# The graph layer turned round: normed tokens as weights, 256 adjacency rows moving, and the linear product afterwards

## The chip, the cores and the metric

The kernel runs on one core of a Trainium2 chip. The metric is the device time of one execution, in microseconds (us). Engines are named as in the profile: PE is TensorE (PEld its weight loads), DVE is VectorE, ACT is ScalarE, POOL is GpSimd, SP is SyncE, which here issues DMAs.

## The reference, cut to what matters

There are 4096 tokens of 256 features and a dense 4096 x 4096 adjacency matrix. One graph layer is followed by one layer of causal attention and a mixture of eight experts, two of them for each token. The change touches the graph layer alone:

```
f = layernorm(x)
h = f @ neigh_W.T
deg = adj.sum(axis=1, keepdims=True) + 1.0
h = adj @ h / deg
x = x + concatenate([f, h], axis=-1) @ lin_W.T
```

With lin_W split into a left half L1 (for f) and a right half L2 (for h), the update is x + f L1 + (adj f M) / deg, with M = neigh_W.T L2 (in the transposes that the code uses). The product with M may be made before the product with adj or after it.

## The kernel before, in words

The graph stage works on row blocks b and source blocks jb of 512 tokens, eight of each. For every pair the 512 x 512 adjacency block, transposed in memory, is loaded (`load`, three buffers) and multiplied with the features of the source block. The product is done by a seven-product scheme (Strassen's, in Winograd's form): the adjacency block is cut into quarters A11 to A22, `halve` makes four sums of them on VectorE (S1, S2, S4, and S3 in place of A21; lines L428 to L431), and the features are cut and combined in the same way (tile g with G11, G12, G21, G22, T1, T2, T3 in the place of G12, and T4; L453 to L456). Each sum tile has two slots, used in turn.

In the kernel before, `features(b)` multiplies the normed tokens, transposed by `turned_x` (L377, copied by L381), with 512 columns at once: M in the left half, L1 in the right (L439). ACT copies the left half of the result into g (L446), VectorE adds the right half to the residual (L449).

`aggregate(b, steps)` is the main loop. For each jb it issues 28 matmuls (L477): seven products, two row tiles t, two halves k of the source tokens. The adjacency piece is the stationary operand (128 x 128) and g the moving one, 128 columns; two of the seven products have a 129th column of ones in g, from which the row sums of the adjacency come out. After the eighth source block the sums are put together from PSUM: an ACT copy (L497) and VectorE operations (L498 to L504), then the degrees (L505 to L507) and the residual (L510), for one t and then the other. The accumulators lie in two PSUM pools of two banks, one pool for each t, so the next row block can only overwrite a bank that has been read.

The order of the work is written out by hand: each engine takes its instructions in the order of the program. The `steps` of a row block are pieces of other work that are put in the middle of a source block. In row block 0 they are `features`, `turned_x`, `halve` and `scales_x` of later blocks. In row block b from 1 on they are the seven or eight parts of `qkv(b - 1)`: `scales` (statistics, and a power on GpSimd, L168 and L169), `norm`, `turn`, four times `rotate` (matmuls L197; ACT's L201, VectorE's L205 and L210, GpSimd's L213 to L217, VectorE's reduction L219 and maximum L220), and four times `turn_heads` (L227 and L232). The last rotation stands in source block 6, the last two turn_heads in source block 7. For b from 1 on, `halve` of the next adjacency block is issued ahead of a source block's matmuls.

After row block 7 the attention stage begins at once on TensorE; it takes over the PSUM banks of the graph stage's pools.

Of the kernel before, what the change touches and what calls it, by code (L numbers as in the profile page):

```python
# [66 lines left out]
def fast_kernel(  # L67
# [170 lines left out]
    with (  # L238
# [20 lines left out]
        for h in range(2):  # L259
# [7 lines left out]
        ml_sb = qT[6]  # L267
        nc.scalar.dma_start(
            ml_sb[:, :, C : 2 * C], lin_t[0:C, :].rearrange("(c p) o -> p c o", p=P)
        )  # L270
# [66 lines left out]
        def fold():  # L337
            for c in range(2):
                pm = p_pj.tile([P, 512], F32, tag="pj", name=f"pm_{c}")
                for k in range(2):  # L340
                    nc.tensor.matmul(
                        pm[:, :C], wn_sb[:, k, c * P : (c + 1) * P], l2_sb[:, k, :],
                        start=(k == 0), stop=(k == 1),
                    )
                nc.scalar.copy(ml_sb[:, c, 0:C], pm[:, :C])
# [14 lines left out]
        g = [gw.tile([P, 7, 2, HC + 1], F32, name=f"g{b}") for b in range(NB)]  # L360
# [5 lines left out]
        AT = {  # L366
            1: (0, 0, HC), 2: (0, HC, HC), 6: (0, 2 * HC, HC), 7: (0, 3 * HC, HC),
            3: (1, 0, HC + 1), 5: (1, HC + 1, HC + 1), 4: (1, 2 * HC + 2, HC),
        }

        def transposed(src, dst):

            for h in range(2):
                tr = p_tr.tile([P, 2, 2, P], F32, tag="tr", name="tr")
                for t in range(2):
                    for c in range(2):
                        nc.tensor.transpose(  # L377
                            tr[:, c, t, :], src[:, 2 * h + t, c * P : (c + 1) * P], ident
                        )
                cols = slice(h * 2 * P, (h + 1) * 2 * P)  # L380
                nc.scalar.copy(dst[:, :, cols], tr.rearrange("p c t i -> p c (t i)"))  # L381

        inputs, turned = {}, {}

        def scales_x(b, at_a_time=TB):
            for t in range(0, TB, at_a_time):
                some = slice(t, t + at_a_time)
                stats(gx, b, range(TB)[some])
                power(rstd[b][:, some], mv[b][:, some, 1:2], 1.0, EPS_LN)
            nc.gpsimd.memset(g[b][:, G22 : T1 + 1, :, HC : HC + 1], 1.0)  # L390

        def normed_x(b, t):
            if t == 0:
                inputs[b] = gx.tile([P, TB, C], F32, tag="f", name=f"f_{b}", bufs=1)
            normed(inputs[b][:, t, :], b, t, rstd[b][:, t])

        def turned_x(b):
            turned[b] = qT[b % 4]
            transposed(inputs.pop(b), turned[b])
# [3 lines left out]
        more = gs.tile([P, 3, 2, 2 * P], F32, name="more_sums")  # L403
        sums_at = [
            tuple(
                t.rearrange("p (k i) -> p k i", k=2)
                for t in (qT[NB - 1][:, 0], qT[NB - 1][:, 1], kT[NB - 1])
# [4 lines left out]
        rows_at = [  # L412
            vv[NB - 1].rearrange("p (r h) c -> p r h c", r=2),
            gs.tile([P, 2, 2, HC], F32, name="rows_sums"),
        ]

        def halve(n):

            if n == NB * NB:
                return  # L420
            a = blocks.pop(n)
            m = {
                f"A{r + 1}{k + 1}": a[:, 2 * k : 2 * k + 2, r * 2 * P : (r + 1) * 2 * P]
                for r in range(2) for k in range(2)
            }
            m["S1"], m["S2"], m["S4"] = sums_at[n % 2]
            m["S3"] = m["A21"]
            nc.vector.tensor_add(m["S1"], m["A21"], m["A22"])  # L428
            nc.vector.tensor_sub(m["S2"], m["S1"], m["A11"])
            nc.vector.tensor_sub(m["S4"], m["A12"], m["S2"])  # L430
            nc.vector.tensor_sub(m["S3"], m["A11"], m["A21"])  # L431
            halves_of[n] = m

        def features(b):
            fT = turned.pop(b)
            for t in range(TB):
                pj = p_pj.tile([P, 512], F32, tag="pj", name=f"pf_{b}_{t}")
                for c in range(2):
                    nc.tensor.matmul(  # L439
                        pj, fT[:, c, t * P : (t + 1) * P], ml_sb[:, c, :],  # L440
                        start=(c == 0), stop=(c == 1),
                    )
                if b + 1 < NB:
                    normed_x(b + 1, t)
                i = t // 2 * 2
                nc.scalar.copy(  # L446
                    g[b][:, i : i + 2, t % 2, 0:HC], pj[:, 0:C].rearrange("p (h c) -> p h c", h=2)
                )
                nc.vector.tensor_add(res[b][:, t, :], res[b][:, t, :], pj[:, C : 2 * C])  # L449
                if b == 0 and t == 1:  # L450
                    halve(0)
            part = [g[b][:, k, :, 0:HC] for k in range(7)]
            nc.vector.tensor_sub(part[T1], part[G12], part[G11])  # L453
            nc.vector.tensor_sub(part[T3], part[G22], part[G12])
            nc.vector.tensor_sub(part[T2], part[G22], part[T1])
            nc.vector.tensor_sub(part[T4], part[T2], part[G21])  # L456

        def aggregate(b, steps):

            acc = [  # L460
                [pool.tile([P, 512], F32, tag="acc", name=f"acc_{b}_{t}_{k}") for k in range(2)]
                for t, pool in enumerate((p_acc0, p_acc1))
            ]
            for jb in range(NB):
# [3 lines left out]
                order = [(p, t) for p in PRODUCTS for t in range(2)]  # L468
                if jb == 0 and b:
                    load_tables(b - 1)  # L470
                if jb == NB - 1 or b and jb == 0:
                    order = [(p, t) for t in range(2) for p in PRODUCTS]
                for i, ((number, left, right), t) in enumerate(order):
                    bank, at, w = AT[number]
                    for k in range(2):

                        nc.tensor.matmul(  # L477
                            acc[t][bank][:, at : at + w], m[left][:, k, t * P : (t + 1) * P],
                            g[jb][:, right, k, 0:w],
                            start=(jb == 0 and k == 0 and number in (1, 3)),  # L480
# [3 lines left out]
                    if i == 6:  # L484
                        for step in steps.get(jb, ()):
                            step()
                load(b * NB + jb + 3)
            for t in range(2):
                p = {
                    number: acc[t][bank][:, at : at + HC] for number, (bank, at, w) in AT.items()  # L490
                }
                rows = rows_at[t]
                deg = gx.tile([P, 2], F32, tag="deg", name=f"deg_{b}_{t}")

                u2 = u4 = rows[:, 0, 1]
                u3 = rows[:, 1, 1]
                nc.scalar.copy(u2, p[1])  # L497
                nc.vector.tensor_add(rows[:, 0, 0], u2, p[2])  # L498
                nc.vector.tensor_add(u2, u2, p[6])
                nc.vector.tensor_add(u3, u2, p[7])  # L500
                nc.vector.tensor_add(u4, u2, p[5])
                nc.vector.tensor_add(rows[:, 0, 1], u4, p[3])
                nc.vector.tensor_sub(rows[:, 1, 0], u3, p[4])
                nc.vector.tensor_add(rows[:, 1, 1], u3, p[5])  # L504
                nc.vector.tensor_scalar_add(deg[:, 1:2], acc[t][1][:, 2 * HC + 1 : 2 * HC + 2], 1.0)  # L505
                nc.vector.tensor_add(deg[:, 0:1], deg[:, 1:2], acc[t][1][:, HC : HC + 1])
                nc.vector.reciprocal(deg, deg)  # L507
                for r in range(2):
                    x1 = res[b][:, 2 * r + t, :]
                    nc.vector.scalar_tensor_tensor(  # L510
                        x1, rows[:, r].rearrange("p h c -> p (h c)"), deg[:, r : r + 1], x1,
                        op0=ALU.mult, op1=ALU.add,
                    )

        def qkv(b):
# [9 lines left out]
            def norm():  # L525
                made["h0"] = gx.tile([P, TB, C], F32, tag="f", name=f"h0_{b}", bufs=1)
                for t in range(TB):
                    normed(made["h0"][:, t, :], b, t, both[b][:, t])
                made["ratio"] = ratio(gx, b)

            def turn():

                made["hT"] = qT[b]
                transposed(made["h0"], made["hT"])
# [14 lines left out]
            def turn_heads(t):  # L549
# [3 lines left out]
            return {  # L553
                0: [scales], 1: [norm], 2: [turn], 3: [lambda: rotate(0)], 4: [lambda: rotate(1)],
                5: [lambda: turn_heads(0), lambda: rotate(2)],
                6: [lambda: turn_heads(1), lambda: rotate(3)],
                7: [lambda: turn_heads(2), lambda: turn_heads(3)],
            }
# [15 lines left out]
        turned_x(0)  # L574
        features(0)
# [10 lines left out]
        aggregate(0, steps)  # L586
        for b in range(1, NB):
            aggregate(b, qkv(b - 1))
# [4 lines left out]
    with (  # L593
# [11 lines left out]
        p_sc = cycle((p_sc0, p_sc1, p_sc2))  # L605
# [1553 lines left out]
```

## Time and profile before

| | |
|---|---|
| Time, median of 3 runs | 1611.35 us (1609.33 to 1614.71) |
| Span of the profiled execution | 1603.0 us |
| Graph stage in it | from the start to 539.6 us |
| TensorE busy | 1588.4 us (99%) |
| VectorE busy | 1025.0 us (64%) |
| One row block from 1 on | 59.3 us, of which VectorE is busy 37.4 us and GpSimd 11.5 us |
| L477, all products | 3584 matmul records of 128 or 129 columns |
| L439, features | 128 matmul records of 512 columns |

An f32 matmul leaves two records, each with its weight load. A record's own duration (275 ns for L477) holds the passage through the array, in which the next record already runs; what a record costs is read from the chain of waits, as the length of a piece over the number of its records. The profile's slices give the busy share of each engine in tenths, for 40 equal parts of the span.

### The profile page before, as it was taken

What the parts mean: (1) busy time and instruction counts of PE and PEld (TensorE: products, weight loads), DVE (VectorE), ACT (ScalarE), POOL (GpSimd) and SP (SyncE); (2) the same over time, 40 slices, a digit from 0 to 9 for tenths busy, and PEclk for the clock granted to TensorE, in tenths of its full rate; (3) what the DMA queues carried; (4) which work ended last, traced back from release to release, by engine and by line L of the source; (5) the groups of instructions that cost most, each with busy time, mean ns of one, the idle gap of its engine ahead of it and who ended that gap; (6) DMA issues with size and microseconds to landing.
All of it is one profiled execution on the core that took longest, in us unless ns stands there. A gap on an engine that the chain in (4) does not pass through costs nothing.

```text
span 1603.0 us, 25842 instructions
## 1 busy us (share of the span) xinstructions
PE 1588.4 (99%) x9996; PEld 1172.1 (73%) x9996; DVE 1025.0 (64%) x2159; ACT 483.8 (30%) x925; POOL 418.3 (26%) x606
## 2 busy tenths in 40 slices
PE   9999999999999999999999999999999999999997
PEld 6779999999999643444343443337889999999997
DVE  5656756656656668789889788794445544343552
ACT  2120110110110445545545545552212222222221
POOL 1001111111111231254453334322422212222213
PEclk9999999999999999999999999999999999999999
DMA  6324434444435000001010001058756777787783
GB/s 230 99 72 145 159 133 146 151 132 161 136 132 165 4 1 1 13 33 36 18 38 28 14 28 38 20 182 235 237 169 199 233 227 251 225 300 248 232 296 67
DMA packets 68005, 209.80 MB, mean 131 GB/s; under 512 B 14688, under 2 KB 46816, under 8 KB 54240
## 3 DMA queue, kind: packets, MB, share of 16 engines
q1 hardware_dynamic: 54608, 190.05, 35.0%
q0 software_dynamic: 12720, 17.47, 5.6%
q8 instruction: 81, 1.33, 0.4%
q10 hardware_dynamic: 544, 0.52, 0.1%
q14 instruction: 52, 0.43, 0.1%
HBM read 180.81 MB, written 31.42 MB: 132 GB/s over the span
## 4 chain that ended last, share of the span: by engine, by line
PE 89%; DVE 7%; ACT 1%; issue 1%; POOL 1%; DMA 0%; SPq 0%; DVEq 0%; POOLq 0%; ACTq 0%
PE acc L477 25%; PE h L1231 20%; PE ya L652 11%; PE sc L617 11%; PE ye_y L1283 5%; DVE sum L640 4%; PE pf L439 3%; PE ye_y L1202 3%; PE pq L197 2%; PE ye_ms L1202 2%; PE po L687 2%; PE tx L1140 1%; ACT pt L622 1%; DVE rden L671 1%; PE trq L227 1%
## 5 line engine op out<-in xcount | busy, mean ns | idle before, releaser
L640 DVE TENSOR_TENSOR sum<-sum,pt 128x1024 f32<-128x1024 f32 (+3 forms) x258 | 295.4, 1145 | 17.2
L622 ACT ACTIVATE pt<-sc 128x1024 f32<-128x1024 f32 (+3 forms) x288 | 252.3, 958 | 173.6 <-PE sc L617 123.8
L477 PE MATMUL acc<-g,a 128*128 128x128 f32 x2048 | 255.9, 275 | 0.0
L617 PE MATMUL sc<-qT_all,kT 64*128 64x512 f32 (+3 forms) x1152 | 250.4, 569 | 1.4 <-ACT pt L622 0.4
L652 PE MATMUL ya<-pt,vv 128*64 128x512 f32 (+3 forms) x1152 | 242.6, 563 | 0.0
L477 PEld LDWEIGHTS acc<-g,a 128*128 128x128 f32 x2048 | 241.9, 192 | 0.0
L1231 PE MATMUL h<-xT,qT_all 128*128 128x256 f32 (+1 forms) x1232 | 221.3, 338 | 0.0
L1231 PEld LDWEIGHTS h<-xT,qT_all 128*128 128x128 f32 x1232 | 196.6, 191 | 20.2 <-issue 1.2
L617 PEld LDWEIGHTS sc<-qT_all,kT 64*128 64x128 f32 x1152 | 103.8, 186 | 141.0 <-issue 106.2
L1238 DVE TENSOR_TENSOR hT<-si,h 128x256 f32<-128x256 f32 (+2 forms) x126 | 62.7, 506 | 189.3 <-ACT si L1237 189.2
L652 PEld LDWEIGHTS ya<-pt,vv 128*64 128x64 f32 x1152 | 76.3, 136 | 146.9 <-issue 139.1
L1303 POOL DMA_INDIRECT acc_dram<-y,rows x57 | 89.7, 1574 | 307.5 <-DVE y L1298 152.3
L1237 ACT ACTIVATE si<-h 128x256 f32<-128x256 f32 (+2 forms) x126 | 57.0, 453 | 278.6 <-PE h L1231 274.6
L1231 PE MATMUL h<-xT,res_all 128*128 128x256 f32 (+1 forms) x616 | 108.2, 334 | 0.0
L1231 PEld LDWEIGHTS h<-xT,res_all 128*128 128x128 f32 x616 | 96.6, 191 | 9.0
L836 POOL DMA_INDIRECT lists<-row,slots x64 | 72.3, 1130 | 115.4 <-issue 114.8
L477 PE MATMUL acc<-g,more_sums 128*128 128x129 f32 (+1 forms) x768 | 101.7, 275 | 0.2 <-DVE more_sums L430 0.2
L477 PEld LDWEIGHTS acc<-g,more_sums 128*128 128x128 f32 x768 | 94.6, 192 | 4.3 <-issue 0.4
L624 POOL TENSOR_SCALAR_AFFINE_SELECT pt<-pt 128x256 f32<-128x256 f32 x64 | 47.6, 770 | 114.1 <-ACT pt L622 113.9
L477 PE MATMUL acc<-g,qT_all 128*128 128x128 f32 (+1 forms) x512 | 74.0, 275 | 0.0
L213 POOL TENSOR_TENSOR ro<-ro,r 128x192 f32<-128x192 f32 x28 | 16.5, 589 | 214.0 <-DVE r L210 214.0
L477 PEld LDWEIGHTS acc<-g,qT_all 128*128 128x128 f32 x512 | 66.4, 192 | 3.9
(275 smaller groups left out, 1960.9 us busy)
## 6 DMA issues: line engine op xcount, KB each, us to landing
a<-in_adj_dram SPq DMA_DIRECT2D x64, 1024.0 KB, 4.9
qT_all<-in_w_dram SPq DMA_DIRECT2D x28, 1408.0 KB, 8.1
res_all<-in_w_dram SPq DMA_DIRECT2D x28, 768.0 KB, 5.3
res_all<-in_w_dram SPq DMA_DIRECT2D x14, 1408.0 KB, 8.4
qT_all<-in_w_dram SPq DMA_DIRECT2D x14, 768.0 KB, 5.1
rows<-lists SPq DMA_DIRECT2D x25, 265.0 KB, 2.9
lists<-pad SPq DMA_DIRECT2D x8, 662.5 KB, 14.9
acc_dram<-res_all SPq DMA_DIRECT2D x8, 512.0 KB, 2.9
```

Source lines behind the costliest of these rows:

```text
L477: nc.tensor.matmul(acc[t][bank][:, at : at + w], m[left][:, k, t * P : (t + 1) * P], g[jb][:, right, k, 0:w], start=(jb == 0 and k == 0 an ...
L617: nc.tensor.matmul(ps[:, j, :w], kT[sb][hd, i * P : (i + 1) * P], qT[b][hd, p, off:], start=True, stop=True,)
L622: nc.scalar.activation(pt[:, :, :w], ps[:, :, :w], AF.Exp, scale=HD ** -0.5)
L640: nc.vector.tensor_add(sums[b, p][:, :, off:], before[:, :, off:], pt[:, :, : 512 - off])
L652: nc.tensor.matmul(accs[b, p][hd, off:], vv[sb][:, i, hd], pt[:, j, : 512 - off], start=(s == 0), stop=(s == TB * b + TB - 1),)
L836: put = nc.gpsimd.indirect_dma_start(out=lists[:, :], out_offset=bass.IndirectOffsetOnAxis(ap=chosen[b][:, k, t, :], axis=0), in_=flats[b] ...
L1202: nc.tensor.matmul(p[number], m[left][:, j, :], m[right][:, j, :], start=(n % 4 == 0 and j == 0), stop=(j == 2), skip_group_check=True,)
L1231: nc.tensor.matmul(ps[:, m % 2, m // 2 - q, :], w13_sb[:, c, m * P : (m + 1) * P], xT[:, c, :], start=(c == 0), stop=(c == 1),)
L1237: nc.scalar.activation(si[:, 0:both, :], ps[:, 0, 0:both, :], AF.Silu)
L1238: nc.vector.tensor_mul(hT[:, q : q + both, :], si[:, 0:both, :], ps[:, 1, 0:both, :])
L1283: nc.tensor.matmul(ps[h if last else 0][:, h, :], hT[:, q, cols], w2_sb[:, q, :], start=(q == 0), stop=(q == NF),)
L1303: put = nc.gpsimd.indirect_dma_start(out=(acc_dram if k < NM - LAST else out)[:, :], out_offset=at, in_=y[:, h, :], in_offset=None, comput ...
```

## The change

The layer is turned round. The normed tokens themselves are put into g (without the multiplication by M) and become the stationary operand, 128 x 128; the adjacency pieces and their sums are the moving operand, 256 rows at once. A source block then has 14 matmuls of 256 columns instead of 28 of 128, and the result is the transposed neighbour sum (features on the partitions). That is what a following product with M needs: `linear`, new, multiplies it with M after the row block is complete, in the next row block's source block 0, and adds it, divided by the degree, to the residual. `features` is left with the product with L1, 256 columns.

Since there is no column of ones any more, the row sums come from GpSimd: after each `halve` it adds S4 and S1 over the source blocks (all_s), at the end of a row block it folds them, TensorE sums over the partitions with 32 columns of ones (`sums`, in source block 7) and turns the result (`degrees`). The steps of `qkv` move one place later: the last rotation stands in source block 7, the last two turn_heads in source block 0 of the next row block. The order of the products in source blocks 0 and 7 follows the PSUM banks. The purpose is to have fewer and longer matmuls for the same arithmetic.

```diff
-        g = [gw.tile([P, 7, 2, HC + 1], F32, name=f"g{b}") for b in range(NB)]
+        g = [gw.tile([P, 7, 2, HC], F32, name=f"g{b}") for b in range(NB)]
...
+        BY_BANK = [next(p for p in PRODUCTS if p[0] == number) for number in (1, 2, 6, 7, 5, 3, 4)]
+        AT = {number: divmod(n, 2) for n, (number, _, _) in enumerate(BY_BANK)}
...
         def normed_x(b, t):
-            if t == 0:
-                inputs[b] = gx.tile([P, TB, C], F32, tag="f", name=f"f_{b}", bufs=1)
-            normed(inputs[b][:, t, :], b, t, rstd[b][:, t])
+            i = t // 2 * 2
+            nc.vector.tensor_scalar(
+                g[b][:, i : i + 2, t % 2, :], res[b][:, t, :].rearrange("p (h c) -> p h c", h=2),
+                mv[b][:, t, 0:1], rstd[b][:, t], op0=ALU.subtract, op1=ALU.mult,
+            )
...
+            jb = n % NB
+            for i, k in ((0, 2), (1, 0)):
+                if jb == 1:
+                    nc.gpsimd.tensor_add(all_s[:, i], sums_at[(n - 1) % 2][k], sums_at[n % 2][k])
+                elif jb > 1:
+                    nc.gpsimd.tensor_add(all_s[:, i], all_s[:, i], sums_at[n % 2][k])
+            if jb == NB - 1:
+
+                ends = all_s[:, :, 0, :]
+                nc.gpsimd.tensor_add(ends, ends, all_s[:, :, 1, :])
+                nc.gpsimd.tensor_add(ends[:, 0], ends[:, 0], ends[:, 1])
...
             acc = [
-                [pool.tile([P, 512], F32, tag="acc", name=f"acc_{b}_{t}_{k}") for k in range(2)]
-                for t, pool in enumerate((p_acc0, p_acc1))
+                pool.tile([P, 2, 2 * P], F32, tag="acc", name=f"acc_{b}_{k}")
+                for k, pool in enumerate((p_acc0, p_acc0, p_acc1, p_acc1))
             ]
...
-                            acc[t][bank][:, at : at + w], m[left][:, k, t * P : (t + 1) * P],
-                            g[jb][:, right, k, 0:w],
+                            acc[bank][:, at, :], g[jb][:, right, k, :], m[left][:, k, :],
...
-                    if i == 6:
+                    if i == 3:
                         for step in steps.get(jb, ()):
                             step()
+                for step in steps.get((jb, "end"), ()):
+                    step()
...
+            u2 = u4 = neighbours[1][:, 0]
+            u3 = neighbours[1][:, 1]
+            nc.scalar.copy(u2, p[1])
+            nc.vector.tensor_add(neighbours[0][:, 0], u2, p[2])
+            nc.vector.tensor_add(u2, u2, p[6])
+            nc.vector.tensor_add(u3, u2, p[7])
+            nc.vector.tensor_add(u4, u2, p[5])
+            nc.vector.tensor_add(neighbours[1][:, 0], u4, p[3])
+            nc.vector.tensor_sub(neighbours[0][:, 1], u3, p[4])
+            nc.vector.tensor_add(neighbours[1][:, 1], u3, p[5])
...
+            def linear():
                 for r in range(2):
+                    pj = p_pj.tile([P, 2, C], F32, tag="pj", name=f"ph_{b}_{r}")
+                    for t in range(2):
+                        for c in range(2):
+                            nc.tensor.matmul(
+                                pj[:, t, :], neighbours[c][:, r, t * P : (t + 1) * P],
+                                m_sb[:, c, :], start=(c == 0), stop=(c == 1),
+                            )
...
+            turns = [lambda t=t: turn_heads(t) for t in range(TB)]
+            rotates = [lambda t=t: rotate(t) for t in range(TB)]
+            return [
+                [scales], [norm], [turn], [rotates[0]], [turns[0], rotates[1]],
+                [turns[1], rotates[2]], [rotates[3]], [turns[2], turns[3]],
+            ]
...
         scales_x(1)
         turned_x(0)
+        halve(0)
         features(0)
...
+        behind, at_end = [], []
+        for b in range(NB):
+            sums, degrees, linear = finish(b)
+            if b:
+
+                steps = {0: behind, (0, "end"): at_end}
+                *amid, behind = qkv(b - 1)
+                for jb, fs in enumerate(amid):
+                    steps[jb + 1] = fs
+            steps[NB - 1] = [sums, *steps[NB - 1]]
+            aggregate(b, steps)
+            at_end = [degrees, linear]
+        for step in (*behind, *at_end):
+            step()
```

## The prediction

> **What bounds the kernel now.** First the page's busy shares and slices:
>
> ```profile
> PE 1588.4 (99%) x9996; PEld 1172.1 (73%) x9996; DVE 1025.0 (64%) x2159; ACT 483.8 (30%) x925; POOL 418.3 (26%) x606
> PE   9999999999999999999999999999999999999997
> PEld 6779999999999643444343443337889999999997
> POOL 1001111111111231254453334322422212222213
> ```
>
> TensorE is never idle. The graph stage is the first 13 or so slices; there its weight loads are nearly as dense as the matmuls, and GpSimd has room. A busy PE need not be at its peak, so I read the chain of waits next, over the graph stage. Columns: start in us, length in us, engine, tile, line, count.
>
> ```profile
> 30.17 6.25 PE acc L477 x56
> 36.42 6.87 PE pf L439 x16
> 43.29 0.88 PE tr L377 x8
> ...
> 512.02 6.25 PE acc L477 x56
> 518.27 0.45 PE trq L227 x4
> 518.72 0.33 PE trq L232 x3
> 519.05 1.32 PE pq L197 x4
> ...
> 1209.40 9.50 PE h L1231 x44
> ```
>
> The chain is TensorE alone, piece after piece: in row block 0 a source block takes 6.25 + 6.87 + 0.87 = 14.0 us, in the others 6.25 us plus a share of the query and key work. So a microsecond of TensorE is a microsecond of the kernel, gained or lost. It also gives prices per record (an f32 matmul is two records): 6.25/56 = 111.6 ns at 128 columns, 6.87/16 = 429.4 ns at 512, and, from the expert stage, 9.50/44 = 215.9 ns at 256.
>
> Then the timeline around one rotation, since the change moves it next to a place where TensorE depends on VectorE:
>
> ```profile
> 520.20 0.61 PE L477 MATMUL acc<-g,more_sums 128*128 128x129 f32 x4
> 520.40 0.27 ACT L201 ACTIVATE first_lg<-pq,ratio 128x8 f32<-128x8 f32 x1 [0.56 <-PE pq L197]
> 520.70 0.56 DVE L205 TENSOR_TENSOR ro<-pq,cos 128x384 f32<-128x384 f32 x1 [1.82 <-ACT first_lg L201]
> ...
> 522.87 0.82 POOL L217 TENSOR_TENSOR r<-ro 128x384 f32<-128x384 f32 x1
> 523.73 0.55 DVE L219 TENSOR_REDUCE nm<-r 128x6 f32<-128x384 f32 x1 [1.94 <-POOL r L217]
> 524.32 0.17 DVE L220 TENSOR_TENSOR norms<-norms,nm 128x6 f32<-128x6 f32 x1
> 524.40 0.69 DVE L428 TENSOR_TENSOR more_sums<-a 128x512 f32<-128x512 f32 x1
> ```
>
> TensorE passes on from pq at 520.20, and VectorE is free of this rotation only at 524.40: 4.2 us later, 1.94 of them idle, because L219 waits for three GpSimd operations and everything else on VectorE queues behind it.
>
> **What the Trainium skill says.** "TensorE: Matmul & The Clock Gate", section "Back-to-back issue gap", gives N/2.4 + 2.5 ns for an isolated warm matmul. Taken twice over the columns, the trace fits with one such floor per record: 2 x 512/2.4 = 426.7 against 429.4, 2 x 256/2.4 = 213.3 against 215.9; at 128 columns it is 106.7 against 111.6, 2 ns above the rule. The same page, "Architectural detail", calls VectorE's queue strict FIFO; L219 and L428 above agree. "GPSIMD Engine Reference", "Key points": GpSimd shares its SBUF interfaces with VectorE and contends with its instructions of two SBUF inputs. The trace agrees: L740, 128x32 with two SBUF inputs, takes 0.87 us while L694 runs on GpSimd and 0.19 at its quickest. "TensorEngine Tiling (Array Packing)", "Key Properties": changing the tiling mode drains TensorE, which bears on the new sums.
>
> **The change part by part.**
>
> Products (L477). 28 matmuls of 128 (some 129) columns per source block become 14 of 256: 1792 records at 215.9 in place of 3584 at 111.6 ns, 386.9 against 400.0 us, **-13.1 us**. All on the path. The arithmetic is the same; what goes is 5 ns per record.
>
> Features (L439). 16 records of 512 columns become 16 of 256 per block: 6.87 to 3.45 us, eight times, **-27.3 us**. But the later product with neigh_W and L2 adds 8 matmuls, 16 records of 256, per row block: 8 x 3.45 = **+27.6 us**. Together nothing: 512 columns are split into two places.
>
> Row sums and degrees. Four 32-column matmuls of 128 columns are 8 records per row block; the same form, L724, takes 0.57 us for 16 until the next matmul starts, so 0.3, plus up to 0.2 for the change of tiling, plus one 0.11 us transpose: 0.6 x 8, **+4.5 us** (2.5 to 9, the upper end if the four don't overlap).
>
> VectorE's own work. Gone are the ACT copies L446 and eight small epilogues' operations; the epilogue becomes seven operations of 128x256, some 0.33 to 0.45 us each, and four of 0.44 for the residual. All of it lies beside TensorE unless named below.
>
> Start. VectorE is what the first products wait for (stats of block 1 are done at 10.9 us). After it: 1.6 us of subtractions, halve(0) at 2.65 (it can't start before its adjacency block lands; the DMA rates summed give 3.9 MB by 13.5 us, what is queued up to and with that block), then four normed tiles and two adds, 2.7 us. That is 19 us for the first product, where it was 19.14. So the 3.4 us saved in features(0) are idle: **+3.4 us** (2 to 4).
>
> Row block 0. TensorE's period falls from 14.0 to 28 x 0.216 + 3.45 + 0.87 = 10.4 us. VectorE's: normed 1.4, adds 1.3, subtractions 1.6, halve 2.65, stats and the wait for GpSimd's power 3.1, together 10.0. GpSimd's two new 128x512 adds come ahead of that power: L217 takes 0.83 us for 384 elements and L694 2.17 for 1024, so 1.1 us each, and the first waits behind S3, which has two SBUF inputs. They end some 2.9 us after S4, where the power now starts 2.4 after it: VectorE needs 10.5. Six or seven periods at 0.1 to 0.2 over, **+1 us** (0 to 6, if contention stretches the adds by half as it does L169, 1.01 to 1.54 us).
>
> First sums. For row block 0, S4 of the last block comes 4.5 us after the last features; 2.9 us of adds and 1.1 for the two folding adds put the sums at 8.5 us or later. TensorE arrives after 12 + 16 records and waits inside its queue, from 6.1 us: **+2.5 us** (0 to 4). In other row blocks the block is halved a whole step earlier, and the adds are done.
>
> **Row block boundaries.** This decides it. rotate(3) now falls into source block 7, after product 7; only 12 records follow it, 2.59 us, and then the next row block's product 1 wants the bank of products 1 and 2 (p_acc0 has two buffers, both in use). That bank is free when VectorE has read p[2], the first vector operation of the epilogue. But the epilogue is queued behind rotate(3)'s reduction: 4.2 us after pq, plus 0.42 for a 128x256 read of PSUM (L449) and some 0.05 for the semaphore: 4.67. TensorE waits 4.67 - 2.59 = 2.1 us. The later banks are read at 0.4 us a step, faster than products of 0.86 us come to them. In the kernel before, only turn_heads stands there, with no VectorE work. Six boundaries (1 to 2 up to 6 to 7) have a rotation ahead of them: **+12.4 us** (0 to 18).
>
> End. After row block 7 nothing but two turn_heads (1.56 us) and a transpose stands between the last product and the new linear product, which needs five epilogue operations: 4.2 + 2.1 us after pq against 4.26 for TensorE: **+2.0 us** (0 to 4). Then attention starts as before.
>
> Sum: -13.1 - 27.3 + 27.6 + 4.5 + 3.4 + 1 + 2.5 + 12.4 + 2.0 = +13.0; 1611.35 + 13.0 = **1624 us**.
>
> **Rivals.**
> 1. The boundaries are hidden: VectorE gets to p[2] in time. The sum loses 12.4 and 2.0: +0 to -1.4, **1610**, no change. For it: VectorE has slack on average (37.4 us busy of 59.3 per row block). Against: it is an order of instructions, not a load, and the order is written out.
> 2. Only the matmul count matters, start and first sums hidden too: -13.1 + 0.3 + 4.5 = -8.3, **1603**, faster. For it: the chain is all TensorE. Against: the start is VectorE's already (the chain shows L428 to L431 and L177 there).
> 3. GpSimd's adds bind: 64 x 2.2 us at half as much again are 210 us; row block 0 becomes VectorE's at 11.5 us, +7, and the rotation chain lengthens by 0.5 at each boundary, +3: **1634**. For it: the measured contention. Against: outside row block 0 the adds end (6.5 us into a step) before the rotation's GpSimd work begins (7.3).
>
> **How the numbers follow.** Forecast 0.70, rival 1 0.13, rival 2 0.08, rival 3 0.09. The forecast's bounds alone give about 1615 to 1632; a boundary wait of half the size would come to 1617. Range 1608 to 1631: it takes in rival 1, leaves out rival 2 and most of rival 3. Faster 0.09, same 0.15 (rival 1 and a little of the forecast), slower 0.76.
>
> **What would show it.** In the profile after: acc pieces of 28 records near 6.05 us; features 16 records near 3.45; the first product near 19 us; steps near 10.5 us in row block 0; ahead of product 1 of row blocks 2 to 7 a gap of 2 us put down to VectorE's first epilogue add, with L219's successor ahead of it; a wait of the sums on GpSimd once. It is wrong if 256-column records take more or less than 216 ns between LDWEIGHTS of g, if the boundary gap is missing, or if GpSimd's adds take far more than 1.1 us.

## The result, and the profile after

| | before | after |
|---|---|---|
| Time, median | 1610.57 us (1609.33 to 1614.71) | 1635.16 us (1630.38 to 1637.06) |
| Ratio, with its 95% interval | | 1.0144 (1.0115 to 1.0173) |
| End of the graph stage in the profile (first attention score) | 539.57 us | 564.77 us |
| Mean granted clock of TensorE | 0.998 | 0.991 |

The changed kernel is slower, by 24.6 us where the prediction had 13.0. The graph stage alone ends 25.2 us later. The two profiles differ by 32.3 us in span; the remaining 7 us lie in the expert stage, in waits that some of the runs below have as well and others have not (4.3 us at L1258, for VectorE's work, which itself had waited for a load of weights). So the graph stage is what has to be explained.

The page of the kernel after, busy shares and two rows of slices:

```profile
PE 1594.9 (98%) x8404; PEld 1144.5 (70%) x8404; DVE 1029.8 (63%) x2055; ACT 473.0 (29%) x893; POOL 591.6 (36%) x726
...
POOL 2336445455464422233544224322522212222213
PEclk9999999999999999999999999999999999999999
```

TensorE issues 1592 records fewer and is busy for 6.5 us more: fewer and longer matmuls are there, and still it loses. GpSimd's slices rise from 1 to between 3 and 6, the row sums. The clock's row shows nothing, in any slice. That row misled: a slice is 40 us long, and what matters here lasts 3.

Next, the waits of TensorE up to the end of the graph stage (total us, times, longest us):

```profile
PE acc L484 <- DVE kT L501: 13.8, 6, 2.3
PE tr L374 <- DVE g L388: 4.3, 2, 4.2
PE degT L517 <- POOL all_s L448: 2.5, 1, 2.5
...
PE ph L539 <- DVE vv L505: 1.2, 1, 1.2
```

Before, the longest wait of TensorE on another engine's work in this stage was 0.2 us, apart from the masks and a load at the start; from 20 us on there was one such wait:

```profile
PE acc L477 <- DVE more_sums L430: 0.2, 1, 0.2
```

Now there are four kinds, and they are the four that the prediction named: six boundaries, the start, the first sums, the end. L501 is the first VectorE operation of the epilogue.

The boundary into one row block, in the timeline after (start, length, engine, line; in brackets the idle time before it and what ended that):

```profile
296.40 1.03 PE L484 MATMUL acc<-a,g 128*128 128x256 f32 x4
...
298.59 0.55 DVE L219 TENSOR_REDUCE nm<-r 128x6 f32<-128x384 f32 x1 [1.95 <-POOL r L217]
...
299.26 0.42 DVE L501 TENSOR_TENSOR kT<-vv,acc 128x256 f32<-128x256 f32 x1
299.73 3.58 PE L484 MATMUL acc<-a,g 128*128 128x256 f32 x8 [2.30 <-DVE kT L501]
303.10 1.17 PE L484 MATMUL acc<-qT_all,g 128*128 128x256 f32 x4
```

The queue is as predicted: L219 waits for GpSimd, L501 stands behind it, product 1 waits for L501. The four records at 296.40 are issued by 296.40 + 4 x 0.215 = 297.26, and the next start at 299.73: 2.47 us of nothing. And then comes what the prediction did not have. The eight records of product 1 take from 299.73 to 303.10, 0.42 us each. The same eight at the boundary of another row block:

```profile
171.17 1.99 PE L484 MATMUL acc<-a,g 128*128 128x256 f32 x8 [2.25 <-DVE kT L501]
```

Eight in 1.99 us, which includes the passage of the last: the ordinary 0.216 us each. The same instructions after nearly the same wait run at half the rate in one place and not in the other. In stretches of 5 us the granted clock shows it (length, PE busy and records, clock, DMA share, GB/s), after:

```profile
20.00:25.00 5.00, 5.00 (x17) 0.65 0.84 291
...
105.00:110.00 5.00, 5.00 (x16) 0.62 0.10 11
...
300.00:305.00 5.00, 5.00 (x17) 0.66 0.47 154
```

A TensorE that is busy for all of the 5 us gets through 17 records instead of 25 or so. Four places have this: the start (8 records, 20.16 to 23.54), after the first sums (13 records, 103.12 to 108.81), and two of the six boundaries (299.73 and 429.96). Above 0.216 us a record they cost 1.65, 2.9, and 1.6 twice; and eight records of another piece between the first sums and 103.12 (p_wo, L328) take 1.46 us where they took 0.81 before. Together that is 8.4 us.

Stretches cut where the clock changes are sharper. The granted clock is one half in four pieces of this stage: from 16.66 us for 6.83 us, from 101.99 for 6.83, from 299.96 for 3.41 and from 429.67 for 3.41. Two of them with the stretch ahead, and then a boundary that has none:

```profile
98.58:101.99 3.41, 0.86 (x12) 1.00 0.27 113
101.99:108.82 6.83, 6.83 (x21) 0.50 0.01 2
...
296.55:299.96 3.41, 1.11 (x6) 1.00 0.44 115
299.96:303.37 3.41, 3.41 (x9) 0.50 0.71 231
...
361.40:364.81 3.41, 1.99 (x10) 1.00 0.26 34
364.81:368.23 3.42, 2.54 (x12) 1.00 0.89 307
```

The four starts lie 25, 58 and 38 times 3.413 us apart. So the half clock comes on a raster, a fixed grid of stretches of 3.41 us that runs on whatever TensorE does, and that tells the two boundaries apart. The wait before 299.73 fell into one stretch of the raster, where TensorE idled for 2.30 us (3.41 less 1.11), and the next stretch had half the clock. The wait before 365.69, just as long, was cut in two by the raster's edge, into 1.42 and 0.88 us, and the clock stayed.

Five of the experiments below also have half-clock pieces; in each of these traces they start at whole multiples of 3.413 us from one another. Over the six traces, 17 of 18 stretches in which TensorE idled (no record in progress) for 1.9 us or more were followed by half the clock (2.02 us was followed by it, 1.97 once not); of those with 0.7 to 1.85 us, two were, one that had half the clock itself and one that holds the sums. The two pieces of 6.83 us, and one more in the first experiment, are two stretches; behind the first sums TensorE was busy in the first of them, and why a second followed is open. This rule is read from the traces; no run was made to test it.

### The profile page after: what moved, and what is told of

Its sections match the earlier page's. It is cut to its first block, busy times and chain, and to the rows that moved or that the text cites. A ratio compares the mean times of both kernels' runs of the same rounds, so it can differ in the third digit from the quotient of the medians.

```text
span 1635.3 us, 22647 instructions
## 1 busy us (share of the span) xinstructions
PE 1594.9 (98%) x8404; PEld 1144.5 (70%) x8404; DVE 1029.8 (63%) x2055; ACT 473.0 (29%) x893; POOL 591.6 (36%) x726
## 3 DMA queue, kind: packets, MB, share of 16 engines
q8 instruction: 68, 1.11, 0.3%
## 5 line engine op out<-in xcount | busy, mean ns | idle before, releaser
L484 PE MATMUL acc<-a,g 128*128 128x256 f32 x1024 | 250.7, 386 | 13.8 <-DVE kT L501 13.8
L484 PEld LDWEIGHTS acc<-a,g 128*128 128x128 f32 x1024 | 197.0, 194 | 48.0 <-DVE kT L501 16.2
L443 POOL TENSOR_TENSOR all_s<-all_s,more_sums 128x512 f32<-128x512 f32 x72 | 106.9, 1497 | 162.7 <-DVE more_sums L435 162.7
L484 PE MATMUL acc<-more_sums,g 128*128 128x256 f32 x512 | 128.0, 383 | 0.0
L484 PEld LDWEIGHTS acc<-more_sums,g 128*128 128x128 f32 x512 | 98.3, 192 | 15.2
L376 ACT COPY qT_all<-tr 128x512 f32<-128x512 f32 x30 | 16.6, 588 | 223.9 <-PE tr L374 223.3
L484 PE MATMUL acc<-qT_all,g 128*128 128x256 f32 x256 | 65.9, 380 | 0.0
```

The costliest lines, as they stand in the source:

```text
L443: nc.gpsimd.tensor_add(all_s[:, i], all_s[:, i], sums_at[n % 2][k])
L484: nc.tensor.matmul(acc[bank][:, at, :], g[jb][:, right, k, :], m[left][:, k, :], start=(jb == 0 and k == 0 and at == 0), stop=(jb == NB - ...
```

## The experiments

Theory A is that the 24.6 us are the predicted waits, a little longer than predicted, plus half-rate matmuls behind some of them. Theory B is rival 3: GpSimd's additions stretch VectorE's work, and everything else follows from that. A third, rival 1's, is that the boundaries cost little and something else is at work. Ratios are to the kernel before, run beside each experiment.

**Take the reduction out of the epilogue's way.** The reduction and maximum of the last rotation (L219, L220) are put off into the next row block's source block 0.

```diff
+        def check():
             nm = pool.tile([P, 6, 1], F32, tag="nm", name=f"nm_{b}_{t}")
             nc.vector.tensor_reduce(nm, sq, AX.X, ALU.add)
             nc.vector.tensor_max(norms, norms, nm.rearrange("p h o -> p (h o)"))
+        if late is None:
+            check()
+        else:
+            late.append(check)
...
-                [turns[1], rotates[2]], [rotates[3]], [turns[2], turns[3]],
+                [turns[1], rotates[2]], [rotates[3]], [lambda: late.pop()(), turns[2], turns[3]],
```

> Only the order of two VectorE instructions changes: the reduction and maximum (L219, L220) of the last rotation of a row block are issued in the next row block, behind the epilogue. Theory (VectorE's queue held by a reduction that waits for GpSimd makes TensorE wait at six boundaries, and two of those waits also cost the clock): product 1 of row blocks 2 to 7 starts some 2.3 us sooner each, 14 us, and no slow records follow there, 3 us: about 1618 us, attention starting near 548 us instead of 564.8. Rival (GpSimd's adds bind the graph stage): TensorE would wait elsewhere for the same time, 1632 us or more.

Measured: 1613.29 us, ratio 1.0021 (1.0009 to 1.0032); the graph stage ends at 543.02, clock 0.995. A boundary in its timeline:

```profile
166.43 2.75 PE L491 MATMUL acc<-a,g 128*128 128x256 f32 x12
166.54 0.41 DVE L508 TENSOR_TENSOR kT<-vv,acc 128x256 f32<-128x256 f32 x1
...
172.20 0.55 DVE L221 TENSOR_REDUCE nm<-r 128x6 f32<-128x384 f32 x1
```

The epilogue's first operation now runs at 166.54, while the last products do, and the twelve records before and after the boundary form one run. All six boundary waits are gone, and so is the wait at the end. 21.75 us of graph stage go with one reduction and its maximum put off. 18.7 of them lie between the first product of row block 1 and that of row block 7: six waits and two slow stretches. 1.8 lie at the end. The other 1.25 come before row block 1: the first adjacency block landed sooner (13.96 instead of 14.82), and the half clock of the start was shorter (3.41 us instead of 6.83). Rival 1 falls, and so does Theory B as the main cause: every addition of GpSimd is still in this kernel.

**Keep the waits, fill them with matmuls.** Matmuls of the identity, whose result nobody reads, are put where TensorE would wait.

```diff
+        def fill(k, name):
+            idle = p_tr.tile([P, 2, 2, P], F32, tag="tr", name=name)
+            for n in range(k):
+                nc.tensor.matmul(idle[:, 0, 0, :], ident, ident, start=True, stop=True)
...
         features(0)
+        fill(19, "fill_start")
...
+            if b == 0:
+                steps[NB - 1].insert(0, lambda: fill(11, "fill_first"))
             aggregate(b, steps)
+            if 0 < b < NB - 1:
+                fill(9, f"fill_{b}")
```

> Adds useless matmuls on TensorE, as many as fit into its known waits (19 at the start, 11 ahead of the first sums, 9 at each of six boundaries), and nothing else. Theory (after a wait TensorE is granted a lower clock for some us, and that is about 8 us of the time): the waits stay, but no acc record takes 0.43 us any more; the granted clock returns to 0.998; about 1627 us. Rival (the slow records only shift work that would have waited anyway): 1635 us; if the fill itself is in the way, more.

Measured: 1625.47 us, ratio 1.0099 (1.0077 to 1.012); graph stage 555.56, clock 0.998. The granted clock of TensorE in this kernel, in two of the stretches shown above:

```profile
105.00:110.00 5.00, 5.00 (x25) 1.00 0.65 192
...
300.00:305.00 5.00, 5.00 (x25) 1.00 0.47 174
```

and its timeline at the start and at a boundary:

```profile
13.87 4.40 PE L512 MATMUL fill_start<-ident 128*128 128x128 f32 x38
...
18.99 1.89 PE L484 MATMUL acc<-a,g 128*128 128x256 f32 x8
...
293.65 1.99 PE L484 MATMUL acc<-a,g 128*128 128x256 f32 x8 [0.32 <-DVE kT L501]
```

Nothing useful was added, and the products come no sooner behind a wait (the boundaries that were at full rate still lie 64.3 us apart); TensorE merely was not idle. No half-clock piece is left in this stage, and 9.2 us of it came back. At the start the first product comes at 18.99 instead of 20.16; 0.4 of that are transposes that no longer run at half rate, and the rest is the landing again. So about 8.5 are the clock, beside the 8.4 counted from the records. This is the only experiment that changes the clock alone, and it separates the two parts of Theory A.

**Leave out GpSimd's additions.** This kernel leaves out the additions of the row sums, so its degrees are a constant's.

```diff
+        nc.gpsimd.memset(all_s, 1.0)
...
-            for i, k in ((0, 2), (1, 0)):
-                if jb == 1:
-                    nc.gpsimd.tensor_add(all_s[:, i], sums_at[(n - 1) % 2][k], sums_at[n % 2][k])
-                elif jb > 1:
-                    nc.gpsimd.tensor_add(all_s[:, i], all_s[:, i], sums_at[n % 2][k])
-            if jb == NB - 1:
...
-                nc.gpsimd.tensor_add(ends, ends, all_s[:, :, 1, :])
-                nc.gpsimd.tensor_add(ends[:, 0], ends[:, 0], ends[:, 1])
```

> Leaves out GpSimd's additions of the row sums (all_s is set to ones once), so the degrees are not the reference's. Theory: only row block 0 feels them: the wait of the first sums (2.7 us), the slow records after it (3 us) and 0.28 us in each of six periods go: about 1628 us; the six waits of 2.3 us at the boundaries stay. Rival (GpSimd's adds through the interfaces it shares with VectorE are the main cause): 1615 us or less, and the boundary waits shrink.

Measured: 1628.48 us, ratio 1.0099 (1.0062 to 1.0135); graph stage 556.04. Its waits have no line for the sums any more, and the boundary line is

```profile
PE acc L474 <- DVE kT L491: 11.5, 6, 1.9
```

The additions are worth 6.7 us of time and 8.7 of graph stage. Of those, 2.5 are the wait of the first sums, 3.5 the slow records behind it and 2.3 the boundaries, where the additions had made the rotation of the source block before end later; 1.1 is row block 0, whose source blocks now take 10.37 us (four of them took 10.66), and 1.1 the start's earlier landing (first product at 19.02); a third slow boundary takes 1.6 back. Theory B has a part, most of it through the waits. Three of these six boundaries show half-rate records, although the longest wait is down to 1.9 us: in these three, all of the wait fell into one stretch of the raster. Its four runs spread as a raster would have it, without proving it: the one of 1619.73 us had a mean clock of 0.996, the one of 1629.33 us 0.992.

**Move the first halving back.** One of the four waits alone: `halve(0)` is issued behind `features(0)`, so that VectorE makes the tokens of the features first.

```diff
-        halve(0)
         features(0)
+        halve(0)
```

> halve(0) is issued after features(0) instead of before it, so that the normed tokens of block 1 need not wait on VectorE behind the first adjacency block's arrival. Theory (order in VectorE's queue): first product at about 15.5 us instead of 20.2, the second features at about 19 instead of 25.3, no slow records at the start: 6 us less, about 1629 us. Rival (the start is bound by the adjacency load itself): first product no earlier than 19 us, within 1 us of 1635.

Measured: 1625.24 us, ratio 1.0104 (1.0078 to 1.0129); graph stage 556.65. The start in its timeline:

```profile
13.61 1.04 PE L374 MATMUL tr<-ident,g 128*128 128x128 f32 x8
14.48 1.89 PE L484 MATMUL acc<-a,g 128*128 128x256 f32 x8
...
18.40 3.62 PE L457 MATMUL pf<-qT_all 128*128 128x256 f32 x16
```

The first product starts at 14.48 instead of 20.16, at the full rate, and the features follow it. Of the 8.1 us of graph stage, 5.3 are the start with its slow records (by the features of block 2, at 30.39 instead of 35.64); one slow boundary fewer (one of six, where after has two) makes 1.6 more, and the half clock behind the first sums, 3.41 us instead of 6.83, another 1.4.

**Move the sums back.** `sums` is issued behind source block 7's products instead of in the middle of them.

```diff
-            steps[NB - 1] = [sums, *steps[NB - 1]]
+            steps[NB - 1, "end"] = [sums]
```

> sums of a row block is issued after the last product of source block 7 instead of after its fourth. Theory: in row block 0 the GpSimd adds are done by then, so the wait of 2.7 us and the slow records after it (3 us) go; elsewhere it only changes places: about 1629.5 us. Rival (VectorE and GpSimd, slowed by each other there, are late for the epilogue anyway): within 1.5 us of 1635.

Measured: 1627.09 us, ratio 1.0114 (1.01 to 1.0129); graph stage 559.85. The wait for the sums is gone. The boundary line of its waits is

```profile
PE acc L484 <- DVE kT L501: 16.1, 7, 2.5
```

where it was 13.8 over six. Six are now 2.5 each, and a seventh, out of row block 0, is 1.1: there the epilogue's first copy waits behind ACT's copy of the sums (L523, which idled 2.88 us), as the next experiment shows for all seven. The gain is 4.9 us of graph stage. 4.6 are the first sums with their slow records, the seventh wait taken off; 1.2 are an earlier start (first product at 19.10) and 0.6 the end; a third slow boundary takes 1.7 back.

**All three edits together.** The reduction put off, the first halving and the sums moved back.

> Three changes of order together: the late check, halve(0) behind features(0), sums after the last product. Theory (the three waits and the lower clock after them are all that the turned layer costs): graph stage ends near 529.5 us (543.0 with the late check, less 8.1 and 5.5), about 1600 us, 0.6% below the kernel before. Rival (with these waits gone another one binds, such as VectorE's period of 10.66 us in row block 0): 1607 us or more.

Measured: 1608.78 us, ratio 1.001 (1.0 to 1.002); graph stage 542.51. The expectation was missed by 9 us: in the graph stage the three together do hardly better than putting off the reduction alone (542.51 against 543.02). Its timeline at a boundary says why:

```profile
158.37 0.43 PE L524 MATMUL degT<-all_s,ones 128*32 128x128 f32 x8
158.89 0.27 ACT L530 COPY degs<-degT 128x128 f32<-128x128 f32 x1 [2.73 <-PE degT L524]
159.05 0.38 ACT L507 COPY vv<-acc 128x256 f32<-128x256 f32 x1
159.47 0.42 DVE L508 TENSOR_TENSOR kT<-vv,acc 128x256 f32<-128x256 f32 x1 [1.29 <-ACT vv L507]
159.94 1.99 PE L491 MATMUL acc<-a,g 128*128 128x256 f32 x8 [1.14 <-DVE kT L508]
```

ACT's copy of the sums (L530) waits for TensorE's sums, and in ACT's queue it stands ahead of the copy L507 that begins the epilogue. The fault is the same as the reduction's, on another engine: a short operation waits for late data in front of the one that frees a bank. Seven waits of 1.1 us, 8.0 in all. None of them was followed by half-rate records.

**The sums behind that copy.** As the last, with `sums` issued after the epilogue's ACT copy.

```diff
             nc.scalar.copy(u2, p[1])
+            for step in steps.get("copied", ()):
+                step()
             nc.vector.tensor_add(neighbours[0][:, 0], u2, p[2])
...
-            steps[NB - 1] = [sums, *steps[NB - 1]]
+            steps["copied"] = [sums]
```

> As the three changes of order together, but sums is issued behind ACT's copy u2 of the epilogue, so that this copy no longer stands behind ACT's copy of the sums. Theory (the seven waits of 1.1 us in the three changes together come from ACT's queue: sums, its copy, u2, then VectorE's first add): they go, the graph stage ends near 534.5 us instead of 542.5, and the time is some 8 us less, 1601 us, 0.5% below the kernel before. Rival (VectorE's first add is late for another reason): graph stage no earlier than 541.

Measured: 1599.96 us, ratio 0.9958 (0.9943 to 0.9973), against 1607.56 for the kernel before beside it: faster than both kernels. Graph stage 533.46, clock 0.998. At the same boundary

```profile
156.98 0.41 DVE L510 TENSOR_TENSOR kT<-vv,acc 128x256 f32<-128x256 f32 x1
157.63 1.99 PE L491 MATMUL acc<-a,g 128*128 128x256 f32 x8
```

there is no wait. The 9.05 us between this and the last are the seven boundaries, 1.2 us each with the restart behind the wait, and 0.6 of a wait ahead of the last linear product.

**Row block 0's VectorE order.** Two versions more put the statistics (`scales_x`) ahead of the halving in row block 0, so that the power on GpSimd comes ahead of its additions, and use the sums in an order that suits (products 1, 2, 4, 5, 6, 3, 7). First on the three edits:

> As the three changes of order together, and in row block 0 the statistics of a later block are taken ahead of halve, with the products that need no sums first (1, 2, 4, then 5, 6, 3, 7), so that VectorE does not idle while GpSimd makes the power. Theory: the period of row block 0 falls from 10.66 to about 10.4 us, 1.5 us less than the three changes alone. Rival (the sums come too late for the products): the same or slower.

Measured: 1608.26 us, ratio 0.9998 (0.9988 to 1.0007); graph stage 541.38, 1.1 us less. Then on the version with the copy first:

> As e9, with the statistics ahead of halve and the products without sums first in row block 0. Theory: 1 us less than e9 (the graph stage of the same pair ended 1.1 us earlier with the sums before ACT's copy), 1600 us. Rival: no difference.

Measured: 1598.89 us, ratio 0.9944 (0.993 to 0.9957); graph stage 532.44, 1.0 us less. A period of row block 0 in its timeline:

```profile
30.16 3.62 PE L464 MATMUL pf<-qT_all 128*128 128x256 f32 x16
...
40.54 3.62 PE L464 MATMUL pf<-qT_all 128*128 128x256 f32 x16
```

That is 10.38 us, against 10.67 in the version without (30.30 to 40.97), and the 10.4 which TensorE needs. The graph stage shows the same 1 us in both pairs; in the times the intervals overlap.

**The boundary wait in the kernel before.** Everything as before, with only the parts of `qkv` one source block later, so that the last rotation stands in source block 7.

```diff
-                0: [scales], 1: [norm], 2: [turn], 3: [lambda: rotate(0)], 4: [lambda: rotate(1)],
...
+                1: [scales], 2: [norm], 3: [turn], 4: [lambda: rotate(0)],
+                5: [lambda: turn_heads(0), lambda: rotate(1)],
+                6: [lambda: turn_heads(1), lambda: rotate(2)],
+                7: [lambda: rotate(3)],
+                8: [lambda: turn_heads(2), lambda: turn_heads(3)],
```

> The kernel before, with the steps of the query and key work moved one source block later as in the change, so that the last rotation stands in source block 7; nothing else of the change. Theory (the place of the rotation alone makes the wait): the epilogue's first four operations are behind L219, TensorE waits some 2.9 us at each of six boundaries, 17 us, a few more if the clock falls: 1627 to 1631 us. Rival (VectorE has slack, and it is the turned epilogue that is late): within 3 us of 1609.

Measured: 1630.56 us, ratio 1.0128 (1.0112 to 1.0144); graph stage 559.43, clock 0.995. A boundary in its timeline:

```profile
181.89 0.55 DVE L219 TENSOR_REDUCE nm<-r 128x6 f32<-128x384 f32 x1 [1.96 <-POOL r L217]
...
183.51 0.29 DVE L501 TENSOR_TENSOR vv<-vv,acc 128x128 f32<-128x128 f32 x1
183.58 1.13 PE L477 MATMUL acc<-g,a 128*128 128x128 f32 x8 [1.95 <-issue]
```

The old arithmetic, with the new place of one rotation, is about as slow as the whole change (here the profile puts the wait down to no releaser, but the reduction stands where it stood). Two of the six boundaries have 3.41 us of half clock behind them. In the kernel before, a boundary (at 183.52) lies inside an unbroken run of products:

```profile
183.08 1.50 PE L477 MATMUL acc<-g,a 128*128 128x128 f32 x12
```

So the turn of the layer in itself did not make the kernel slower. Where it put the rotation did for the most part, and where it put the first halving and the sums did for the rest.

## Why the prediction was right and wrong

Its direction, its four waits and its bound (TensorE's chain) were right. Its sum was too small, by 11.6 us of time, and the time lies above the range. By its own steps, each in the graph stage (us):

| step | predicted | measured |
|---|---|---|
| products | -13.1 | -13.2 |
| features | -27.3 | -27.4 |
| linear | +27.6 | +27.6 |
| row sums and degrees | +4.5 | +5.1 |
| start | +3.4 | +4.4 |
| row block 0 | +1 | +1.1 |
| first sums | +2.5 | +2.7 |
| six boundaries | +12.4 | +14.8 |
| end | +2.0 | +2.0 |
| half-rate records behind the waits | no term | +8.4 |
| sum | +13.0 | +25.5, for 25.2 in the profile |

The row sums are eight times 0.36 us until the next record and 0.11 for a transpose, and in seven row blocks 0.2 more, because the record ahead of the sums and the first query record behind them take 0.1 us longer each (the prediction had allowed up to 0.2 for the change of tiling). The end is one wait of 1.2 us and several shorter ones.

**Right.** The prices per record held: 256 columns cost 0.216 us, and the features piece in the timeline of the kernel after

```profile
46.04 3.62 PE L457 MATMUL pf<-qT_all 128*128 128x256 f32 x16
49.49 1.32 PE L374 MATMUL tr<-ident,g 128*128 128x128 f32 x8
...
56.70 3.62 PE L457 MATMUL pf<-qT_all 128*128 128x256 f32 x16
```

takes 49.49 - 46.04 = 3.45 us; from one features piece to the next are 10.66 us, where TensorE's own work is 10.4. Rival 2's -8.3, what the change would bring if its waits were hidden, is close to the 7.6 us that the version with the copy first gains (6.1 in the graph stage). The mechanism of the boundary, one reduction in VectorE's queue that waits for GpSimd, was right to the line, as putting it off and moving it in the kernel before both show.

**The step that failed** is the sum itself: it says "Sum: -13.1 - 27.3 + 27.6 + 4.5 + 3.4 + 1 + 2.5 + 12.4 + 2.0 = +13.0", each wait priced at its own length. The waits also lower the clock of the records that follow, and there was no term for that, nor in the range. Of the 12.2 us of graph stage that the sum missed, 8.4 are this; 2.4 are the boundaries and 1.0 the start. Filled waits give about 8.5 us back. The Trainium skill has the rule: "TensorE: Matmul & The Clock Gate", section "What's actually happening", gives the array half its clock after at least one idle window of about 3.4 us, on a free-running window. The prediction took from this page the issue gap and the order of VectorE's queue, not the clock. This case's trace agrees on the half (0.42 against 0.216 us a record), on the length of the window (3.41 us) and on its running freely (starts at whole multiples of 3.413 us). On how idle a window has to be the measurement decides: about 1.9 us of its 3.41 were enough. That is why a gap of 2.47 us was punished at two boundaries of six.

**The mis-sized terms.** A boundary is 2.47 us, not 2.1. The 0.37 is GpSimd's doing: L219 of the third rotation idles up to 3.8 us because its GpSimd operations queue behind the additions, so the halving behind it, and the last rotation, come later; without the additions the longest wait was 1.9. The prediction had held against rival 3 that the additions end before the rotation's GpSimd work begins; here they do not. The start was priced at 19 us for the first product. It was 20.16 in the profile after, where the adjacency block landed at 14.82, and 18.99 to 19.30 in four other profiles with the same order, where it landed at 13.9 to 14.0. There the term is right; what it costs depends on a landing that moves by 0.9 us, and on transposes ahead of the product that ran at half rate (0.4 us in the profile after).

The first sums came for the reason given, and with the right size by luck. In the timeline of the kernel after:

```profile
94.36 0.69 DVE L435 TENSOR_TENSOR more_sums<-a,more_sums 128x512 f32<-128x512 f32 x1
95.20 3.25 POOL L443 TENSOR_TENSOR all_s<-all_s,more_sums 128x512 f32<-128x512 f32 x2 [5.66 <-DVE more_sums L435]
97.43 1.57 DVE L434 TENSOR_TENSOR qT_all<-qT_all,a 128x512 f32<-128x512 f32 x1
98.53 1.59 POOL L447 TENSOR_TENSOR all_s<-all_s 128x512 f32<-128x512 f32 x1
100.20 1.05 POOL L448 TENSOR_TENSOR all_s<-all_s 128x256 f32<-128x256 f32 x1
101.31 0.42 PE L517 MATMUL degT<-all_s,ones 128*32 128x128 f32 x8 [2.55 <-POOL all_s L448]
```

An addition takes 1.6 us beside VectorE where the prediction had 1.1, and L434, 0.69 us when alone, takes 1.57. From S4 (L435) to the end of the additions are 6.2 us where 4.0 were set; but S4 came 2.9 us after the last features (they end at 92.1), where 4.5 were set. The two errors nearly cancel, and the wait is the predicted 2.5.

**Rivals.** Rival 1 is refuted by the boundary waits and by what putting off the reduction gives. Rival 3 came to the right time (1634) by the wrong way: it had 7 us in row block 0, where 1.1 were found, and without the additions only 6.7 us come back.

## What to carry to other kernels

Price a wait of TensorE of about 2 us or more at its length plus, possibly, one stretch of 3.41 us at half the clock behind it, which is 1.7 us more (an estimate: half of 3.41); whether it falls due depends on how the wait lies on the raster. Look for it in short stretches, because the mean and the slices of 40 us hide it. When work is moved, ask of each engine's queue at the new place what stands behind an operation that waits for another engine: here a reduction, a halving and a set of sums in the wrong place turned a gain of 7.6 us into a loss of 24.6, with every engine but TensorE idle for over a third of the time. A change that looks bad may hold a good part in a bad place; moving the place alone in the old kernel tells them apart.

## What the runs showed of the hardware

- The half clock comes in stretches of 3.41 us, at whole multiples of 3.413 us within a trace, and 17 of 18 stretches with 1.9 us or more of idle TensorE were followed by it (six traces).
- Counted by waits: behind all seven at the start or for the first sums (2.5 to 4.2 us); behind 11 of 30 boundary waits of about 2 us (2 of 6 after, 3 of 6 without the additions, 1 of 6 and 3 of 6 with the halving and the sums moved, 2 of 6 in the kernel before with the late rotation); behind none of fifteen of 1.1 us (one with the sums moved, seven each in the two versions with the three edits and the sums ahead of the copy). A boundary's lasts 3.41 us, that of the start or the first sums 3.41 or 6.83.
- Matmuls of no use keep the clock up: 168 extra records in 8 places, no half-clock piece in the graph stage any more, and the mean clock rises from 0.991 to 0.998.
- GpSimd and VectorE stretch each other: with two SBUF inputs, 128 x 512, GpSimd's addition takes 1.26 us at its quickest and 1.6 beside VectorE, and VectorE's operation goes from 0.69 to 1.57 or more. "GPSIMD Engine Reference", section "Key points", of the Trainium skill says that these contend, without a size.
- The weight load of a matmul that waits is not made ahead of it: at the first sums it idles 2.95 us and starts with its matmul.

```profile
101.31 0.16 PEld L517 LDWEIGHTS degT<-all_s,ones 128*32 128x32 f32 x8 [2.95 <-POOL all_s L448]
```
